# The reduced adjacency of a graph kernel: one wide product for up to four blocks of the unturned removal

## The chip, the cores and the metric

The kernel runs on one core of one Trainium2 chip. The metric is the device time of one execution in microseconds. The profile shows the core's engines: PE (TensorE's products, with PEld for its weight loads), DVE (VectorE), ACT (ScalarE), POOL (GpSimd) and SP, which here only issues DMAs.

## The reference, cut to what matters

Sixteen graphs of 1024 nodes with 64 features go through four layers. The first layer drops some neighbours and then takes, for every node and feature, weighted quantiles over the neighbours that are left; the other three layers are message passing, a second message passing and an attention. The change is in how the first layer's reduced adjacency is built:

```python
adj_ = jnp.where(eye, 1.0, adj)
neigh = (adj_ > 0) & ~eye
ni = neigh.astype(jnp.int32)
rank = jnp.cumsum(ni, axis=-1) - ni
nb = ni.sum(-1)
skip = jnp.maximum(jnp.where(nb > T, (nb + K - 1) // K, 1), 1)
sk = skip[:, :, None]
rem = neigh & (sk > 1) & (rank % sk == sk - 1) & mask[:, :, None]
rem = rem | jnp.swapaxes(rem, 1, 2)
adj_d = jnp.where(rem, 0.0, adj_)
nd = adj_d > 0
```

An edge is taken out when either of its two rows takes it out, so each block of the result needs the removals of its own row and those of the mirrored block, turned.

## The kernel before

The graphs go through in eight pairs. For a pair there are three kinds of work. `neighbours` builds the reduced adjacency of each of its two graphs, stored turned (`ndT`, L935 to L958), and counts its rows (L962). `sort_pair` sorts the pair's features on DVE (L791 to L793, then backwards L824 to L837). `select` reads both and finds the quantiles: products `comb` (L1120) of the reduced adjacency with weight tables `wt` (made on DVE at L998), then signs on ACT (L1175), maxima on DVE (L1191) and a second set of products `cand` (L1220). After it come `extras` and `layers` (the four layers' dense work of both graphs, with the attention at L1579 to L1609).

So the time has two kinds of stage in turn. In a selection stage PE, ACT and DVE work for `select` of pair k, and DVE also does the forward part of the sort of pair k+1. In a layer stage, the layers of pair k stand beside `neighbours` and the rest of the sort for pair k+1. The first 275 us hold `neighbours` and the sort of pair 0; the last pair's layers stand alone.

The order on each engine is not written out by hand. A scheduler places all instructions by priorities and modelled costs, and every engine then works through its own list in order. A kernel with fewer or shorter instructions at one place therefore gets another order around it.

In `neighbours`, each graph is cut into 8 x 8 blocks of 128 x 128. Rows of blocks t = 0 to 7 are handled in turn: ACT makes the row's removals `rem[:, t]` in three passes (L931, L932, L933), and then PE builds all blocks whose later index is t: the column of blocks (j, t) for j up to t, and the row (t, i) for i below t. A block is the sum, in PSUM, of three products: the turned neighbours (`ni` as stationary side against an identity), less the turned removals (`rem` against minus the identity, `minus_b`), less the removals of the mirrored block, which need no turning (`minus_b` as stationary side against `rem`). Diagonal blocks get the identity added. Up to four blocks share one PSUM tile `pk` of 512 columns, and ACT writes them out with a ReLU into `ndT` (L958). There are two such tiles (`bufs=2` of the pool `nbp`), shared with the transposes of the adjacency at L908.

The names of the layer stage that the prediction uses: L1460 are dense products with two weight tiles, L1469 and L1575 make the source side of the attention, L1579 and L1582 its destination side, L1595 and L1596 are the attention's exponential and sum, L1485 its gather products, L1607 turns the sum back and L1609 adds it to the features.

Of the kernel before, what the change touches and what calls it, by code (L numbers as in the profile page):

```python
# [9 lines left out]
F32 = mybir.dt.float32  # L10
# [7 lines left out]
AF = mybir.ActivationFunctionType  # L18
# [5 lines left out]
P = 128  # L24
# [18 lines left out]
def gnn_stack(ctx, tc, x, adj, nodemask, w, out):  # L43
# [10 lines left out]
    nc = tc.nc  # L54
# [10 lines left out]
    ident_b = const.tile([P, P], BF16, name="ident_b")  # L65
# [112 lines left out]
    minus_b = const.tile([P, P], BF16, name="minus_b")  # L178
# [519 lines left out]
    while size <= N:  # L698
        j = size // 2
# [182 lines left out]
    def neighbours(b, ndT, row10, qb, qz, nb, nbp):  # L882

        mask = maskf[:, b * NT : (b + 1) * NT]
        HT = NT // 2
        dq, coef = row10[:, :, :3], row10[:, :, 3:9].rearrange("p t (k s) -> p t k s", s=2)
        pad = 32
        wide = nb.tile([P, NT, pad + N], F8, name="ni")
        nc.gpsimd.memset(wide[:, :, pad - 1 : pad], 0.0)
        ni = wide[:, :, pad:]  # L890
        rem = nb.tile([P, NT, N], F8, name="rem")
        for t0 in range(0, NT, HT):
            cum = nb.tile([P, HT, N], F16, name="cum")
            for t in range(t0, t0 + HT):
                a = nb.tile([P, N], F32, name="a", bufs=2)
                nc.sync.dma_start(a, adj[b, t * P : (t + 1) * P, :])
                nc.vector.tensor_single_scalar(ni[:, t, :], a, 0.0, op=ALU.is_gt, saturate=False)
                nc.gpsimd.tensor_mul(  # L898
                    ni[:, t, t * P : (t + 1) * P], ni[:, t, t * P : (t + 1) * P], offdiag, saturate=False
                )  # L900

                nc.vector.tensor_tensor_scan(  # L902
                    cum[:, t - t0, :], ni[:, t, :], wide[:, t, pad - 1 : pad - 1 + N], 0.0, op0=ALU.add, op1=ALU.add
                )
                for q in range(0, NT, 4):
                    pt = nbp.tile([P, 4, P], F32, name="pk")
                    for k in range(4):
                        nc.tensor.transpose(pt[:, k, :], a[:, (q + k) * P : (q + k + 1) * P], ident)  # L908
                    at = nb.tile([P, 4, P], F32, name="at", bufs=3)
                    nc.scalar.copy(at, pt)  # L910
                    nc.scalar.dma_start(
                        a_d[b % 4, q : q + 4, :, t * P : (t + 1) * P].rearrange("j p n -> p j n"), at
                    )


            sk = nb.tile([P, 4, HT], F32, name="sk")
            nc.vector.tensor_tensor(sk[:, 2, :], cum[:, :, N - 1], ni[:, t0 : t0 + HT, N - 1], op=ALU.add)
            nbi = nb.tile([P, HT], I32, name="nbi")
            nc.vector.tensor_scalar_add(nbi, sk[:, 2, :], 2.0)
            nc.vector.tensor_single_scalar(nbi, nbi, 2, op=ALU.logical_shift_right)  # L920
            nc.vector.tensor_single_scalar(sk[:, 0, :], sk[:, 2, :], 2 * MAX_DEGREE, op=ALU.is_gt)
            nc.vector.tensor_mul(sk[:, 0, :], sk[:, 0, :], mask[:, t0 : t0 + HT])
            nc.vector.tensor_copy(sk[:, 1, :], nbi)
            nc.vector.scalar_tensor_tensor(sk[:, 1, :], sk[:, 1, :], 1.0, sk[:, 0, :], op0=ALU.add, op1=ALU.mult)
            nc.vector.tensor_scalar(sk[:, 2, :], sk[:, 1, :], -3.0, 4.0, op0=ALU.mult, op1=ALU.add)
            nc.vector.tensor_scalar_add(sk[:, 1, :], sk[:, 1, :], -1.0)
            nc.vector.scalar_tensor_tensor(sk[:, 3, :], sk[:, 1, :], -1.0, sk[:, 1, :], op0=ALU.mult, op1=ALU.mult)
            for t in range(t0, t0 + HT):
                k = t - t0
                sq = nb.tile([P, N], F32, name="sq")  # L930
                nc.scalar.activation(sq, cum[:, k, :], AF.Square, bias=sk[:, 2, k : k + 1], scale=1.0)  # L931
                nc.scalar.activation(sq, sq, AF.Square, bias=sk[:, 3, k : k + 1], scale=1.0)  # L932
                nc.scalar.activation(rem[:, t, :], sq, AF.Relu, bias=one, scale=-1.0, saturate=False)  # L933


                for blocks, to in (
                    ([(j, t) for j in range(t + 1)], ndT[:, : t + 1, t * P : (t + 1) * P]),
                    ([(t, i) for i in range(t)], ndT[:, t, : t * P].rearrange("p (i n) -> p i n", n=P)),
                ):
                    for n, (j, i) in enumerate(blocks):  # L940
                        if n % 4 == 0:
                            pk = nbp.tile([P, 4, P], F32, name="pk")
                        terms = [
                            (ni[:, i, j * P : (j + 1) * P], ident_b),
                            (rem[:, i, j * P : (j + 1) * P], minus_b),
                            (minus_b, rem[:, j, i * P : (i + 1) * P]),
                        ]
                        if i == j:
                            terms.append((ident_b, ident_b))
                        last = n % 4 == 3 or n == len(blocks) - 1  # L950
                        for m, (lhs, rhs) in enumerate(terms):
                            nc.tensor.matmul(  # L952
                                pk[:, n % 4, :], lhs, rhs, start=(n % 4 == 0 and m == 0),
                                stop=(m == len(terms) - 1 and last),
                            )
                        if last:
                            n0, m = n - n % 4, n % 4 + 1
                            nc.scalar.activation(to[:, n0 : n + 1, :], pk[:, :m, :], AF.Relu, saturate=False)  # L958
        pn = nbp.tile([P, 4, P], F32, name="pk")[:, 0, :NT]
        for i in range(NT):  # L960
            for j in range(NT):
                nc.tensor.matmul(  # L962
                    pn[:, i : i + 1], ndT[:, j, i * P : (i + 1) * P], ones_b[:, 0:1],
                    start=(i == 0 and j == 0), stop=(i == NT - 1 and j == NT - 1),
                )
        nc.gpsimd.tensor_copy(row10[:, :, 9], ids)

        last = nb.tile([P, NT], F32, name="last")
        nc.vector.tensor_scalar_add(last, pn, -1.0)
        lasts = last.rearrange("p (t o) -> p t o", o=1).to_broadcast([P, NT, 3])  # L970
        fr = nb.tile([P, 2, NT, 3], F32, name="fr")
        fi = nb.tile([P, NT, 3], I32, name="fi")
        nc.vector.tensor_mul(fr[:, 0], lasts, taus)
        nc.vector.tensor_scalar_add(fi, fr[:, 0], -0.4)
        nc.vector.tensor_copy(fr[:, 1], fi)
        nc.vector.tensor_sub(dq, lasts, fr[:, 1])
        nc.vector.tensor_scalar(qb, dq, -2048.0, -2048.0, op0=ALU.mult, op1=ALU.add)
        nc.vector.tensor_scalar(qz, dq[:, :, 0], -1.0, 1.0, op0=ALU.mult, op1=ALU.add)
        nc.vector.tensor_sub(fr[:, 0], fr[:, 0], fr[:, 1])
        nc.vector.tensor_mul(coef[:, :, :, 1], fr[:, 0], shares)  # L980
        nc.vector.tensor_sub(coef[:, :, :, 0], shares, coef[:, :, :, 1])
# [635 lines left out]
    def prepare(pr, nb, nbp):  # L1617

        made = []
        for i in range(2):  # L1620
            made.append((
                ndp.tile([P, NT, N], F8, name=f"ndT{i}"), ndp.tile([P, NT, 10], F32, name=f"row10{i}"),
                ndp.tile([P, NT, 3], F32, name=f"qb{i}"),
                ndp.tile([P, NT], F32, name=f"qz{i}"),
            ))
            neighbours(pr * 2 + i, *made[i], nb, nbp)
        return made
# [17 lines left out]
    for pr in range(pairs):  # L1645
# [17 lines left out]
        with ExitStack() as beside:  # L1663
# [5 lines left out]
            else:  # L1669
                nb_, nbp_ = side_pools()  # L1670
                nb, nbp = beside.enter_context(nb_), beside.enter_context(nbp_)
# [69 lines left out]
```

## Time and profile before

| what | value |
|---|---|
| median of 3 runs | 5758.06 us (5743.28 to 5765.65) |
| the profiled execution's own time | 5775.25 us |
| its span, first to last instruction | 5773.4 us |
| mean granted TensorE clock | 0.852 |
| PE busy | 4354.5 us, 75% |
| PE weight loads busy | 2724.9 us, 47% |
| DVE busy | 4997.9 us, 87% |
| ACT busy | 3813.2 us, 66% |
| POOL busy | 166.5 us, 3% |
| PE products, and as many weight loads | 45010 |

Busy time is a mean over stages. PE's products are pipelined, so that the length shown for one of them overlaps with the next one's; what a product costs is read from a run of them: length of the run by number. The view of busy time by stage gives, for a stretch of time, how long each engine was busy in it and with how many instructions. The chain of waits goes back from the last instruction to what released it each time; a line's share of it is time in which that line alone decided.

| the changed products before (L952) | count | mean length, ns | idle time of PE before them, us |
|---|---|---|---|
| turned neighbours, `ni` | 1024 | 247 | 108.0 |
| turned removals, `rem` stationary | 1024 | 251 | 175.6, waiting for L933 |
| unturned removals, `minus_b` stationary | 1024 | 251 | 0.0 |
| identity on the diagonal | 128 | 269 | 0.0 |

### The profile page before, as it was taken

To read this page: it belongs to the slowest core of one execution; us is meant where nothing else is said; L and a number is where in the kernel's file an instruction comes from. 1 tells how busy PE (TensorE), PEld (TensorE's weight loads), DVE (VectorE), ACT (ScalarE), POOL (GpSimd) and SP (SyncE) were. 2 spreads that over 40 slices of the span, in tenths; PEclk is the share of its full clock that TensorE was granted. 3 is DMA by queue.
4 is the path that set the end of the run, shared out by engine and by line. 5 is a ranking of instruction groups with operands and counts; after the bars stand their busy time and mean duration, and the time that the engine had idled before them with its cause. 6 is when DMAs were issued, how large, how long until landed. Compare 5 with 4: busy or idle time off the path is not lost.

```text
span 5773.4 us, 114332 instructions
## 1 busy us (share of the span) xinstructions
PE 4354.5 (75%) x45010; PEld 2724.9 (47%) x45010; DVE 4997.9 (87%) x13239; ACT 3813.2 (66%) x5763; POOL 166.5 (3%) x292
## 2 busy tenths in 40 slices
PE   1488677886778957788588885788767886779956
PEld 1355443554435544455434554355543554435642
DVE  9899888998889987999879988799888998878754
ACT  2587657775586855868568666687667866477835
POOL 3000000000000000000000000000000000000000
PEclk9699878997789978899779996899868997789967
DMA  4401264013731047210561115611255013630030
GB/s 129 127 27 41 88 208 134 26 37 107 227 96 35 28 133 232 68 37 23 158 225 53 41 45 175 199 38 40 82 173 173 28 40 90 212 113 18 10 101 5
DMA packets 519813, 551.45 MB, mean 96 GB/s; under 512 B 263297, under 2 KB 413057, under 8 KB 519265
## 3 DMA queue, kind: packets, MB, share of 16 engines
q1 hardware_dynamic: 376864, 459.65, 25.5%
q10 hardware_dynamic: 140064, 81.84, 4.6%
q8 instruction: 355, 5.82, 0.4%
q0 software_dynamic: 2336, 2.57, 0.2%
q14 instruction: 194, 1.58, 0.1%
HBM read 360.17 MB, written 183.76 MB: 94 GB/s over the span
## 4 chain that ended last, share of the span: by engine, by line
PE 34%; DVE 32%; ACT 19%; DMA 10%; issue 4%; POOL 0%; SPq 0%; ACTq 0%; DVEq 0%; POOLq 0%
PE comb L1120 11%; ACT sign L1175 6%; DVE y L1191 5%; PE cand L1220 5%; PE comb L1311 3%; PE bank L1485 3%; DVE cand L1228 3%; DMA a_d<-at 2%; ACT y L1128 2%; DVE cum L902 2%; DMA adjT<-a_d 2%; DVE s L793 1%; DVE s L792 1%; PE pk L952 1%; DVE swapped L791 1%
## 5 line engine op out<-in xcount | busy, mean ns | idle before, releaser
L1120 PE MATMUL comb<-wt,ndT 128*128 128x512 fp8e5 x6144 | 1435.6, 385 | 136.3 <-ACT sign L1175 112.1
L1128 ACT ACTIVATE y<-comb,qb 128x512 int16<-128x512 f32 x1152 | 743.5, 711 | 497.2 <-PE comb L1120 497.2
L1120 PEld LDWEIGHTS <-ndT 128*128 128x128 fp8e5 x6144 | 589.3, 98 | 852.9 <-issue 222.2
L1175 ACT ACTIVATE sign<-comb,lower 128x1024 fp8e5<-128x1024 int16 (+1 forms) x640 | 694.1, 1085 | 0.0
L1175 ACT ACTIVATE sign<-comb,half 128x1024 fp8e5<-128x1024 int16 (+1 forms) x640 | 688.9, 1076 | 0.0
L1220 PE MATMUL cand<-vtab,sign 128*128 128x48 f16 (+1 forms) x18432 | 668.4, 191 | 25.1 <-DVE agg L1097 15.2
L1220 PEld LDWEIGHTS <-sign 128*128 128x128 fp8e5 x18432 | 641.7, 96 | 85.1 <-issue 23.9
L1191 DVE TENSOR_TENSOR y<-y 128x512 uint16<-128x512 uint16 (+5 forms) x896 | 670.1, 790 | 10.5 <-PE comb L1173 10.0
L1228 DVE COPY_PREDICATED cand<-w_f,cand 128x256 f32<-128x256 uint16 (+1 forms) x1536 | 532.7, 378 | 84.1 <-PE cand L1220 81.7
L1173 PE MATMUL comb<-ident_b,y 128*128 128x128 bf16 x4608 | 307.0, 218 | 102.2 <-ACT sign L1175 70.2
L910 ACT COPY at<-pk 128x512 f32<-128x512 f32 x256 | 147.2, 585 | 351.6 <-PE pk L908 177.2
L952 PE MATMUL pk<-minus_b,rem 128*128 128x128 bf16 x1024 | 231.4, 251 | 175.6 <-ACT rem L933 175.6
L1173 PEld LDWEIGHTS <-y 128*128 128x128 bf16 x4608 | 284.8, 97 | 127.2 <-issue 127.1
L952 PE MATMUL pk<-ident_b,ni 128*128 128x128 bf16 x1024 | 227.0, 247 | 108.0 <-ACT ndT L958 63.4
L902 DVE TENSOR_TENSOR_SCAN cum<-ni 128x1024 f16<-128x1024 fp8e5 x128 | 292.3, 2284 | 17.7 <-POOL ni L898 14.4
L1485 PE MATMUL bank<-att,hs 128*64 128x512 f32 x512 | 195.7, 876 | 143.5 <-ACT hs L1601 143.5
L908 PE MATMUL pk<-ident,a 128*128 128x128 f32 x1024 | 188.0, 330 | 144.8 <-DMA a<-in_adj_dram 92.0
L998 DVE TENSOR_SCALAR wt<-node 128x2048 uint8<-128x2048 f16 x224 | 263.3, 1219 | 21.9 <-PE comb L1311 21.9
L1485 PE MATMUL bank<-adjT,nd 128*64 128x512 f32 x896 | 255.5, 638 | 29.7 <-DMA adjT<-a_d 29.2
L792 DVE TENSOR_TENSOR s<-s 128x384 f32<-128x384 f32 (+4 forms) x440 | 263.2, 598 | 0.0
L793 DVE TENSOR_TENSOR s<-s 128x384 f32<-128x384 f32 (+4 forms) x440 | 262.1, 596 | 0.0
L1186 DVE TENSOR_SCALAR y<-y 128x4608 int16<-128x4608 int16 x128 | 173.6, 1356 | 97.6 <-ACT y L1128 96.7
(382 smaller groups left out, 8340.5 us busy)
## 6 DMA issues: line engine op xcount, KB each, us to landing
adjT<-a_d SPq DMA_DIRECT2D x336, 512.0 KB
a<-in_adj_dram SPq DMA_DIRECT2D x128, 512.0 KB
a_d<-at ACTq DMA_DIRECT2D x256, 256.0 KB
m_d<-swapped SPq DMA_DIRECT2D x104, 512.0 KB
swapped<-m_d SPq DMA_DIRECT2D x104, 512.0 KB
n_d<-nat SPq DMA_DIRECT2D x128, 128.0 KB
x_d<-xr SPq DMA_DIRECT2D x48, 256.0 KB
comb_x<-x_d ACTq DMA_DIRECT2D x24, 512.0 KB
```

Source lines behind the costliest of these rows:

```text
L792: nc.vector.tensor_tensor(to_lo, lo, hi, op=ALU.max)
L793: nc.vector.tensor_tensor(to_hi, lo, hi, op=ALU.min)
L902: nc.vector.tensor_tensor_scan(cum[:, t - t0, :], ni[:, t, :], wide[:, t, pad - 1 : pad - 1 + N], 0.0, op0=ALU.add, op1=ALU.add)
L952: nc.tensor.matmul(pk[:, n % 4, :], lhs, rhs, start=(n % 4 == 0 and m == 0), stop=(m == len(terms) - 1 and last),)
L1120: nc.tensor.matmul(pw, ndT[:, j, t * P : (t + 1) * P], wt[1 + g8][:, j].rearrange("p w c -> p (w c)"), start=(j == 0), stop=(j == NT - 1),)
L1128: nc.scalar.activation(y[:, 0, chunks, at : at + 8 * d_].rearrange("p q (w d) -> p q w d", d=d_), pw.rearrange("p (w q d) -> p q w d", w=8 ...
L1173: nc.tensor.transpose(pt[:, q - q0, :], y[:, 0, q, :].bitcast(BF16), ident_b)
L1175: nc.scalar.activation(signs[tl][s][:, q0:q1, :], pt.bitcast(I16), AF.Sign, bias=before[s], scale=-1.0, saturate=False,)
L1191: nc.vector.tensor_tensor(v[:, :, :, :n], v[:, :, :, :n], v[:, :, :, n : 2 * n], op=ALU.max)
L1220: nc.tensor.matmul(cand[:, e, at : at + 12 * d_].rearrange("p (d l) -> p d l", l=12), signs[tl][sec][:, chunk, :], tab[:, q, :, half_ * 12 ...
L1228: nc.vector.copy_predicated(v[:, :, :, dst : dst + k], mk.to_broadcast([P, 2, C // 2, k]), v[:, :, :, frm : frm + k])
L1485: nc.tensor.matmul(po[to : to + C, :], lhs, rhs[:, f * HALF : (f + 1) * HALF], start=(j == 0), stop=(j == NT - 1))
```

## The change

The third product of each block is taken out of the loop over blocks. For each PSUM tile there is now one product with `minus_b` as stationary side and the removals of all its blocks, up to 512 columns, as moving side. It is the first of the tile and starts the accumulation; the other products follow and add to it.

```diff
-for blocks, to in (
-    ([(j, t) for j in range(t + 1)], ndT[:, : t + 1, t * P : (t + 1) * P]),
-    ([(t, i) for i in range(t)], ndT[:, t, : t * P].rearrange("p (i n) -> p i n", n=P)),
+for blocks, to, less in (
+    ([(j, t) for j in range(t + 1)], ndT[:, : t + 1, t * P : (t + 1) * P], rem[:, : t + 1, t * P : (t + 1) * P]),
+    (
+        [(t, i) for i in range(t)], ndT[:, t, : t * P].rearrange("p (i n) -> p i n", n=P),
+        rem[:, t, : t * P].rearrange("p (i n) -> p i n", n=P),
+    ),
 ):
-    for n, (j, i) in enumerate(blocks):
-        if n % 4 == 0:
-            pk = nbp.tile([P, 4, P], F32, name="pk")
-        terms = [
-            (ni[:, i, j * P : (j + 1) * P], ident_b),
-            (rem[:, i, j * P : (j + 1) * P], minus_b),
-            (minus_b, rem[:, j, i * P : (i + 1) * P]),
-        ]
-        if i == j:
-            terms.append((ident_b, ident_b))
-        last = n % 4 == 3 or n == len(blocks) - 1
-        for m, (lhs, rhs) in enumerate(terms):
-            nc.tensor.matmul(
-                pk[:, n % 4, :], lhs, rhs, start=(n % 4 == 0 and m == 0),
-                stop=(m == len(terms) - 1 and last),
-            )
-        if last:
-            n0, m = n - n % 4, n % 4 + 1
-            nc.scalar.activation(to[:, n0 : n + 1, :], pk[:, :m, :], AF.Relu, saturate=False)
+    for n0 in range(0, len(blocks), 4):
+        four = blocks[n0 : n0 + 4]
+        m = len(four)
+        pk = nbp.tile([P, 4, P], F32, name="pk")
+        nc.tensor.matmul(pk[:, :m, :], minus_b, less[:, n0 : n0 + m, :], start=True, stop=False)
+        for n, (j, i) in enumerate(four):
+            terms = [
+                (ni[:, i, j * P : (j + 1) * P], ident_b),
+                (rem[:, i, j * P : (j + 1) * P], minus_b),
+            ]
+            if i == j:
+                terms.append((ident_b, ident_b))
+            for k_, (lhs, rhs) in enumerate(terms):
+                nc.tensor.matmul(
+                    pk[:, n, :], lhs, rhs, start=False, stop=(n == m - 1 and k_ == len(terms) - 1)
+                )
+        nc.scalar.activation(to[:, n0 : n0 + m, :], pk[:, :m, :], AF.Relu, saturate=False)
```

## The prediction

> **What bounds the kernel now.** I read the page's chain of waits first, then busy time by stage, then the pieces of the chain that hold the changed line, and last the waits around it.
>
> ```profile
> span 5773.4 us, 114332 instructions
> ...
> PE 34%; DVE 32%; ACT 19%; DMA 10%; issue 4%; POOL 0%; SPq 0%; ACTq 0%; DVEq 0%; POOLq 0%
> PE comb L1120 11%; ACT sign L1175 6%; DVE y L1191 5%; PE cand L1220 5%; PE comb L1311 3%; PE bank L1485 3%; DVE cand L1228 3%; DMA a_d<-at 2%; ACT y L1128 2%; DVE cum L902 2%; DMA adjT<-a_d 2%; DVE s L793 1%; DVE s L792 1%; PE pk L952 1%; DVE swapped L791 1%
> ...
> L952 PE MATMUL pk<-minus_b,rem 128*128 128x128 bf16 x1024 | 231.4, 251 | 175.6 <-ACT rem L933 175.6
> ```
>
> No engine bounds the whole: the end is set by a chain that changes engine all the time, and the changed line, L952, holds 1% of it, about 58 us (between 29 and 87 by the rounding).
>
> ```profile
> 979.00:1360.00 381.00, 330.54 (x3854) 210.19 (x3853) 352.00 (x911) 277.81 (x453) 2.64 (x4) 0.94 0.10 31
> 1360.00:1683.00 323.00, 216.62 (x1782) 129.57 (x1781) 266.82 (x732) 199.88 (x271) 12.72 (x24) 0.74 0.59 183
> 1683.00:2057.00 374.00, 324.14 (x3848) 206.93 (x3846) 352.43 (x914) 276.81 (x451) 2.51 (x4) 0.96 0.10 32
> 2057.00:2382.00 325.00, 217.52 (x1778) 129.64 (x1779) 265.96 (x732) 200.13 (x271) 12.87 (x24) 0.75 0.58 181
> ...
> sum 2519.00, PE 300.91 PEld 241.46; mean PE 37.61 PEld 30.18
> ```
>
> The rows are stages: bounds, length, then busy time of PE, weight loads, DVE, ACT, POOL, the granted clock, DMA. A selection stage (375 us and more) and a stage of layers (about 320) alternate, seven times. L952 runs only in the layer stages and in the first 275 us. In a layer stage PE is busy for two thirds, DVE for five sixths: no engine is full, and what counts is who waits for whom. The last row is from the same view for L952 alone, over these eight stretches: it keeps PE busy for 300.9 us, so 58/301 = 19% of it lies on the chain.
>
> ```profile
> 163.55 2.33 PE pk L952 x20
> ...
> 300.82 5.33 PE comb L1120 x24
> ...
> 2828.53 2.21 PE pk L952 x19
> ...
> 2869.65 1.33 PE pk L952 x22
> ```
>
> These pieces of the chain give paces. A 128-column product of L952 takes 1.33/22 = 60.5 ns in a stretch at full clock and 2.33/20 = 117 ns where the clock is about half (granted 0.55 to 0.63 in the first stage). A 512-column product with an fp8 moving side takes 5.33/24 = 222 ns, or 55.5 per 128 columns. The group's mean of 251 ns is the length of one pipelined product; it isn't its price.
>
> **The change part by part.** *Removed:* 1024 products of 128 columns and their weight loads (64 blocks for each of 16 graphs). *Added:* 352 wide ones, 22 a graph: ten of 512 columns, four each of 384, 256 and 128. That is 672 products fewer, but the same 64 x 128 columns a graph. At full clock the saving is 1024 x (60.5 - 55.5) = 5.1 us of PE. At half clock, where no 512-column price is shown, twice 222 gives 111 per 128 columns: 1024 x (117 - 111) = 6.1 us. With 19% on the chain: **-1 us**. Upper bound of the gain: each of the 672 products worth a whole pace, 41 to 79 us of PE, of which 19% is 8 to 15 us. I take the low end, as the wide row is of the same engine and the same column count.
>
> One rule would say more. The Trainium skill, "TensorE: Matmul & The Clock Gate", section "Back-to-back issue gap", gives about 81 ns at 128 columns and about 131 at 512 for streams of load and product. With it 82.9 us would go and at most 352 x 131 = 46.1 come back, so 37 us of PE or 7 on the chain. This trace has 222 ns for the 512-column product, so the rule isn't followed.
>
> *The wait at the head of a group.* The block's `ni` product came first and needed no `rem`; the wide product comes first now and needs the fresh `rem` row, ACT's L933. Behind it stand the group's other products, and whatever layer work follows on PE; ACT's eviction L958 waits for the group.
>
> ```profile
> L952 PE MATMUL pk<-rem,minus_b x1024: 216/219/314, 105.0 to 5129.8; 128*128 128x128 fp8e5 x171
> ...
>   ACT rem L933: 373.3, 116
> ```
>
> PE waits for `rem` anyway, 58 times for a product (175.6 us) and 58 for a weight load. In the order of the program at most two `ni` products stand before such a wait. They move behind it: 58 x 2 x 60.5 to 117 = 7 to 14 us of PE, at 19% **+1 to +3 us**; where the scheduler had put nothing before the wait it is 0. I take +1. *Evictions* keep their number and shapes (352): 0; what covers this is only that ACT's work is unchanged. No DMA is added or removed.
>
> *The order.* The scheduler reorders around the shorter product list, and this is worth more than the products. Reading both programs' instruction orders: the first selection is unchanged on PE. In the old order the selection of pair 1 differs from those of pairs 2 to 5, which are alike; in the new one DVE's order from pair 1 on is the same in every cycle. The old pair-1 stage took 381 us against 374 and 375 in pairs 2 and 3: **-6.5 us**, if the order is what made it long.
>
> In each layer stage of the new order the neighbours' last products and their count (L962) stand before the second graph's attention instead of inside it, and four weight pieces (L998), not three, stand before the final sum L1609.
>
> ```profile
> 3035.39 0.17 DVE L1582 TENSOR_SCALAR fdst<-bank 128x8 f32<-128x8 f32 x1 [3.91 <-PE bank L1579]
> ...
> 3077.53 0.69 DVE L1609 TENSOR_TENSOR nd<-bank,xs 128x512 f32<-128x512 f32 x1 [1.38 <-PE bank L1607]
> ...
>   PE bank L1579: 25.0, 10
> ...
>   PE bank L1607: 12.2, 10
> ```
>
> The bracket is DVE's idle time before the instruction, the two last rows its totals for L1582 and L1609. DVE's stall at the stage's last L1609 is 1.51, 0.80, 1.24, 1.38, 0.50, 0.94 and 0 us in the seven stages, 6.4 in all. One more weight piece before it (1.2 us of DVE) covers it: **-6.4 us**. Late next are the weight pieces themselves, which DVE does one after the other, so nothing of it comes back.
>
> At L1582 I can't tell the sign. Between the second graph's layer-3 dense and the L1579 that DVE awaits, PE had 18 products of L952 and will have 17 + 4 + 8 = 29. Gain end: both waits vanish, 25.0 + 12.2 = 37 us (31 more than counted). Loss end: 11 more products at 117 ns, 1.3 us, and one more wait for an eviction, up to 3.4 us (the longest such wait of PE in one layer stage), so 4.7 us in each of seven stages, 33 us. I take 0, being about as near to one end as to the other.
>
> **Sum:** -1 + 1 - 6.5 - 6.4 = -13, with rounding **-14 us** against the span of 5773.4, so 5759.4. The profiled execution was 15 us above the median of the runs, 5758.06; scaled by 5759.4/5773.4 the forecast is **5744 us**, -0.24%.
>
> **The rivals.** *One: the second graph's chain queues behind the neighbours (slower).* Place: PE between L1460 and L1579 in every layer stage, with DVE's attention waiting at L1582. For it: the row of 3.91 us shows that DVE has nothing else to do there, and 29 products stand in front in place of 18. The Trainium skill's page named above, section "Step-by-step: what each phase is for", speaks for it too: only weight loads are pulled ahead, products stay in program order, so a product that waits holds all behind it; the rows only show PE idle at `rem`. Against it: the products moved forward were due later in the same stage. Price: 4.7 x 7 = 33 us, so 5777; it decides from 2 us a stage, and from 6.1 us a stage the kernel is over 0.5% slower. *Two: the earlier neighbours free the attention of its waits.* The 31 us above vanish as well: 5713. For it: DVE idles 55 us of a layer stage of 321. Against it: the waits at L1582 come from the second graph's own dense chain, which stays. *Three: PE's instruction count is what costs.* All 672 products lie on the path at a pace each, 41 to 79 us, middle 60: 5698. Against it: the row of 222 ns, and 1% of the chain. *That the change doesn't do what it says* can be excluded: the built program has the 352 wide products.
>
> **How the numbers follow.** Forecast 0.50 (its own range 5728 to 5762, from the pair-1 and L1609 terms being nothing or double), rival one 0.22, two 0.23, three 0.05. The range 5700 to 5788 takes in both ends of the L1582 term, 5713 and 5777, with some 11 us each for the spread of the runs shown (5743 to 5766). About 0.5%, 29 us, is what a measurement of this kernel can tell from no change. Below 5729: rival two 0.19, three 0.04, the forecast 0.06, so 0.29. Above 5787: half of rival one, 0.11, and 0.05 for a layer order that costs at places I haven't priced, 0.16. The rest, 0.55, is within.
>
> **What would show it.** In the profile after: 352 products of the wide form, the 512-column one at about 222 ns in dense stretches, and no 251 ns saved for each that went. The selection of pair 1 near 375 us. The last L1609 of a stage without a PE wait. L1582's wait for L1579: under 10 us in all speaks for rival two, 50 or more for rival one. Layer stages of 312 us or less, or 326 and more, would make the prediction wrong, since the sum leaves them within 2 us of 320. So would a selection stage that changes anywhere but in pair 1, as no changed line runs there.

## The result, and the profile after

| | kernel before | changed kernel |
|---|---|---|
| median of 20 runs, us | 5762.50 (5743.28 to 5777.65) | 5771.01 (5764.34 to 5787.46) |
| ratio, 95% interval | | 1.0023 (1.0013 to 1.0033) |
| span of the profiled execution, us | 5773.4 | 5766.4 |

The changed kernel is slower by 0.23%, about 13 us; 14 us less were forecast. The two profiles say the opposite of the medians: the profiled execution of before stood near the top of its range, that of the changed kernel in the lower half of its own. The executions of one kernel spread over 20 to 47 us, so two spans can't be set against each other here. Single stretches can, where they come back alike in every stage and every profile.

From the page of the changed kernel: the span, the chain of waits by engine and by line, and the two groups of the changed products (count, busy us, mean ns, idle time before them).

```profile
span 5766.4 us, 113021 instructions
...
PE 35%; DVE 29%; ACT 21%; DMA 10%; issue 3%; SPq 0%; POOL 0%; ACTq 0%; DVEq 0%; POOLq 0%
PE comb L1121 11%; ACT sign L1176 6%; DVE y L1192 5%; PE cand L1221 5%; PE bank L1486 4%; PE comb L1312 4%; DMA a_d<-at 3%; DVE cand L1229 3%; ACT y L1129 2%; DVE cum L902 2%; DMA adjT<-a_d 2%; DMA a<-in_adj_dram 2%; DVE wt L999 2%; ACT att L1596 2%; DVE s L793 1%
...
L947 PE MATMUL pk<-rem,minus_b 128*128 128x512 fp8e5 (+3 forms) x352 | 134.2, 383 | 214.8 <-ACT rem L933 174.1
...
L956 PE MATMUL pk<-minus_b,rem 128*128 128x128 bf16 x1024 | 187.7, 249 | 58.8 <-ACT rem L933 58.8
```

The 352 wide products are there (L947), and the two other products of a block are at L956; from L960 on every line number is one higher than before. The changed lines are no longer among those that the chain's row names. The chain itself is as mixed as it was.

In the answers on waits, for the lines of the layer stage that the prediction named (idle us of DVE before the line, and how often), before:

```profile
  PE bank L1579: 25.0, 10
...
  PE bank L1607: 12.2, 10
...
  ACT att L1595: 54.6, 49
```

and after:

```profile
  PE bank L1580: 11.2, 13
...
  PE bank L1608: 9.3, 4
...
  ACT att L1596: 71.6, 47
```

The waits for the attention's destination side (L1582, now L1583) and for the last transposes (L1609, now L1610) became shorter, by 13.8 and 2.9 us. DVE then waits that much longer for the attention's exponentials (L1596, now L1597): the three together were 91.8 us and are 92.1. Other profiles agree: 92.0 in a second one of the changed kernel (10.7, 9.1 and 72.2), 89.8 to 95.8 in five more of the kernel before. A wait that only moves to a later line of the same stage gives no time back.

### The profile page after: what moved, and what is told of

The parts are those of the page before. It is cut to its first block, busy times and chain, and to the rows that moved or that the text cites. A ratio compares the mean times of both kernels' runs of the same rounds, so it can differ in the third digit from the quotient of the medians.

```text
span 5766.4 us, 113021 instructions
## 1 busy us (share of the span) xinstructions
PE 4325.9 (75%) x44338; PEld 2688.1 (47%) x44338; DVE 5003.6 (87%) x13239; ACT 3813.5 (66%) x5763; POOL 168.6 (3%) x292
## 4 chain that ended last, share of the span: by engine, by line
PE 35%; DVE 29%; ACT 21%; DMA 10%; issue 3%; SPq 0%; POOL 0%; ACTq 0%; DVEq 0%; POOLq 0%
PE comb L1121 11%; ACT sign L1176 6%; DVE y L1192 5%; PE cand L1221 5%; PE bank L1486 4%; PE comb L1312 4%; DMA a_d<-at 3%; DVE cand L1229 3%; ACT y L1129 2%; DVE cum L902 2%; DMA adjT<-a_d 2%; DMA a<-in_adj_dram 2%; DVE wt L999 2%; ACT att L1596 2%; DVE s L793 1%
## 5 line engine op out<-in xcount | busy, mean ns | idle before, releaser
L947 PE MATMUL pk<-rem,minus_b 128*128 128x512 fp8e5 (+3 forms) x352 | 134.2, 383 | 214.8 <-ACT rem L933 174.1
L956 PE MATMUL pk<-minus_b,rem 128*128 128x128 bf16 x1024 | 187.7, 249 | 58.8 <-ACT rem L933 58.8
```

## The experiments

The instruction order of the changed kernel differs from that of before in three places that can be had one by one, since the scheduler reacts to single tiles of the products. *Y*: the layer stages, where neighbours' last products and the end of the sort stand elsewhere around the attention. *Z*: the second products of pair 1's selection. *X*: the backward exchanges of the sort on DVE, some loads on SP, and, as it turned out, a handful of products of the layer stage on PE. The variants keep the old product (`old`) for some tiles:

```diff
+old = <condition>
+if not old:
     nc.tensor.matmul(pk[:, :m, :], minus_b, less[:, n0 : n0 + m, :], start=True, stop=False)
...
     (rem[:, i, j * P : (j + 1) * P], minus_b),
 ]
+if old:
+    terms.append((minus_b, rem[:, j, i * P : (i + 1) * P]))
...
-    pk[:, n, :], lhs, rhs, start=False, stop=(n == m - 1 and k_ == len(terms) - 1)
+    pk[:, n, :], lhs, rhs, start=(old and n == 0 and k_ == 0), stop=(n == m - 1 and k_ == len(terms) - 1)
```

| kernel | condition for the old product | wide products | order | ratio to before, 95% |
|---|---|---|---|---|
| a_again | never | 352 | X, Y, Z | 1.0027 (1.0012 to 1.0042) |
| order_only | not (b odd and t in (4, 5)) | 56 | Y, Z | 0.9998 (0.9980 to 1.0016) |
| products_only | b odd and t in (4, 5) | 296 | X, Z | 1.0036 (1.0021 to 1.0051) |
| image0_only | b odd | 176 | X | 1.0022 (1.0009 to 1.0036) |
| b_again | always | 0 | as before | 1.0002 (0.9987 to 1.0017) |
| image0_kept | not (b even and t >= 2) | 152 | as before | 0.9984 (0.9967 to 1.0000) |
| exch_order | not (b even and t in (1, 4)) | 40 | X | 1.0025 (1.0009 to 1.0040) |
| no_exch | b even and t == 1 | 336 | Y in part, Z | 0.9980 (0.9964 to 0.9996) |

**First four: order or products?** The theory was that the loss comes from the layer stages' new order, the rival that the products themselves cost it.

a_again: 

> The changed kernel once more, unaltered, for a second profile and as the yardstick on the same chip as the next three. Both theories expect the ratio already measured, 1.0023 (1.0013 to 1.0033), some 8 to 19 us above the kernel before. By the theory of the order (the new place of the second image's products has the layer stage issued in another order, and that order is the dearer one), the layer stages of pairs 0 to 6 in this profile are again about 302 to 306 us with more of them near 306 than near 301, and the selection of pair 1 again some 10 us shorter than the 397 us before. By the theory of the products (the 352 wide products and their wait at the head of a group cost the time themselves) the loss is spread over all stages in which neighbours' products run.

order_only: 

> Only tiles 4 and 5 of the second image of each pair have the wide product: 7 wide products a pair, 56 in all, in place of 20 narrow ones; the other 864 of 1024 narrow products stay. The instruction order of the layer stages and of pair 1's selection becomes that of the changed kernel (19 of TensorE's other 41,535 instructions stand elsewhere than there by more than two places, against 1082 from the kernel before); only the sort's exchanges on VectorE keep the order of before. Theory of the order: the loss is there nearly whole, ratio 1.0010 to 1.0035 (5768 to 5783 us if the kernel before takes 5762). Theory of the products: 56 of 352, so 16% of the loss, ratio 1.0000 to 1.0006.

products_only: 

> The reverse: every product is wide but those of tiles 4 and 5 of the second image of each pair (296 wide products, 160 narrow ones left of 1024). The layer stages keep the order of the kernel before; pair 1's selection has the order of the changed kernel, and so have the sort's exchanges. Theory of the order: without the dearer layer stages the gain in pair 1's selection (some 10 us of the 12 that the two profiles show) is what is left, ratio 0.9975 to 0.9995, layer stages near 301 to 305 us as before. Theory of the products: 296 of 352, so 84% of the loss, ratio 1.0008 to 1.0030.

image0_only: 

> Only the first image of each pair has the wide products (176 of 352). Layer stages and all selections keep the order of before; only the sort's exchanges and, with them, some loads on SP stand a few places elsewhere (805 of VectorE's 13,887 instructions by more than two places). Theory of the order: nothing that matters is moved, ratio 0.9990 to 1.0007, and pair 1's selection stays near 397 us. Theory of the products: half of the loss, ratio 1.0006 to 1.0017.

My theory fell. order_only, with the layer stages' order of the changed kernel, loses nothing; products_only and image0_only lose as much as the changed kernel or more. Two things speak against the plain rival too: 176 wide products cost about as much as 352, and what the three slow kernels share besides wide products is order X.

**Next four: products or exchanges?** In X a backward exchange and some loads stand 3 to 30 places elsewhere. Tiles 1 and 4 of the first image, 5 wide products a pair, are enough for it (exch_order), and it goes when tile 1 alone is left old (no_exch).

b_again: 

> The kernel before once more, unaltered, as its own measure: a ratio whose interval holds 1 (every theory), and a second profile, to see whether the 397 us of pair 1's selection come back or belonged to that one execution.

image0_kept (152 wide products, not the 160 that the text says): 

> Wide products in tiles 2 to 7 of the first image of each pair alone: 160 of the 176 that image0_only had, and every other engine instruction in the order of the kernel before (VectorE 7 of 13,887 moved by more than two places, TensorE none, SP 11 DMAs of 1663). The sort's exchanges, which image0_only and products_only had moved, stay. Theory of the products, which the last four kernels left standing: 160 of 176 of image0_only's loss, ratio 1.0008 to 1.0030. Theory of the exchanges (the loss belongs to the sort's exchanges and the loads on SP issued in another order, which the changed kernel, products_only and image0_only share and order_only has not): ratio 0.9990 to 1.0008.

exch_order: 

> Wide products only in tiles 1 and 4 of the first image of each pair: 5 a pair, 40 in all, in place of 96 narrow ones. The sort's exchanges on VectorE and the 4x24 loads of vtab on SP stand as in image0_only (25 of 13,887 VectorE instructions and one DMA of 1663 differ from it by more than two places), the layer stages as before. Theory of the exchanges: the whole loss of image0_only, ratio 1.0010 to 1.0035. Theory of the products: 40 of 176 of it, ratio 0.9997 to 1.0008.

no_exch: 

> The changed kernel, with tile 1 of the first image of each pair alone put back to narrow products (336 of 352 wide products stay). That gives the sort's exchanges and the loads on SP their order of before; the layer stages have an order of their own, between the two kernels' (465 of TensorE's instructions moved from before, 646 from the changed kernel). Theory of the exchanges: no loss, ratio 0.9975 to 1.0007, about 14 us under the changed kernel. Theory of the products: 336 of 352 of the loss, ratio 1.0012 to 1.0040.

The three variants came out on the side of the theory of the exchanges (image0_kept, at 0.9984, a little under its 0.9990 to 1.0008), and none on that of the products: 40 wide products with order X lose 0.25%, 152 with the old order and 336 without X lose nothing. So the loss goes with X. What in X it is, the layer stages show. From the timeline of PE: start, length, line, operation, count, and in brackets PE's idle time before it. First the kernel before, pair 2:

```profile
2208.15 2.08 PE L1469 MATMUL bank<-srcT,l0w_t 64*128 64x512 f32 x4 [0.57 <-ACT srcT L1436]
2210.16 1.11 PE L1432 MATMUL bank<-ident,nd 128*128 128x128 f32 x4
2211.20 0.60 PE L1449 MATMUL bank<-l0b,ones 3*128 3x512 bf16 x1
2211.73 2.82 PE L1504 MATMUL bank<-l0w,two 128*128 128x64 f32 x12
2214.35 2.02 PE L1443 MATMUL bank<-hT,l1w_d 128*128 128x512 f32 x2
2216.30 0.60 PE L1449 MATMUL bank<-l1b,ones 3*128 3x512 bf16 x1
2216.83 1.11 PE L1504 MATMUL bank<-l0w,two 128*128 128x64 f32 x4
```

and the changed kernel, pair 2:

```profile
2191.03 2.07 PE L1470 MATMUL bank<-srcT,l0w_t 64*128 64x512 f32 x2
2193.03 1.11 PE L1433 MATMUL bank<-ident,nd 128*128 128x128 f32 x4
2194.08 2.07 PE L1470 MATMUL bank<-srcT,l0w_t 64*128 64x512 f32 x2
2196.09 0.60 PE L1450 MATMUL bank<-l0b,ones 3*128 3x512 bf16 x1
2196.62 0.69 PE L1505 MATMUL bank<-l0w,two 128*128 128x64 f32 x2
2197.10 2.02 PE L1444 MATMUL bank<-hT,l1w_d 128*128 128x512 f32 x2
2199.05 0.60 PE L1450 MATMUL bank<-l1b,ones 3*128 3x512 bf16 x1
2199.59 3.25 PE L1505 MATMUL bank<-l0w,two 128*128 128x64 f32 x14
```

These are the second image's layer-0 products (`halves_of(l0w1_t, ...)`, which uses L1469 too). One product takes rows 0 to 63 of the contraction, the other rows 64 to 127, each recorded as two instructions. Next to each other they took 2.08 us together. With the four transposes of the first image between them, each took 2.07 us. So they ran side by side as neighbours in PE's list, and one after the other with other products between them. In the Trainium skill, "TensorEngine Tiling (Array Packing)", section "Key Properties", tiles of the array are said to work independently of each other; 2.08 us for two against 2.07 for one agrees.

The views of busy time agree, each from the start of the pair to the end of the last of these 28 records, first before, then the changed kernel. The columns are bounds, length, busy time of PE, weight loads, DVE, ACT and POOL, then the granted clock:

```profile
2208.15:2217.94 9.79, 9.79 (x30) 5.58 (x31) 3.00 (x7) 5.75 (x9) 1.62 (x3) 0.50 0.19 55
...
2191.03:2202.84 11.81, 11.81 (x29) 6.09 (x30) 4.78 (x10) 6.15 (x9) 1.98 (x3) 0.50 0.15 48
```

The same 28 records stand in both (a product of the neighbours overlaps the bounds here and there), at the same clock, so the 2 us are the pair's. PE has no gap in this stretch, and DVE waits for its end. From the timeline of DVE, its two instructions at `x1` (L1511, now L1512), first image and second image of pair 2, before:

```profile
2202.07 0.69 DVE L1511 TENSOR_TENSOR xs<-bank,mask 128x512 f32<-128x512 f32 x1 [2.86 <-PE bank L1504]
...
2217.99 0.69 DVE L1511 TENSOR_TENSOR xs<-bank,mask 128x512 f32<-128x512 f32 x1 [6.77 <-PE bank L1504]
```

and after:

```profile
2185.02 0.69 DVE L1512 TENSOR_TENSOR xs<-bank,mask 128x512 f32<-128x512 f32 x1 [2.85 <-PE bank L1505]
...
2202.87 0.69 DVE L1512 TENSOR_TENSOR xs<-bank,mask 128x512 f32<-128x512 f32 x1 [6.89 <-PE bank L1505]
```

From one to the other, 15.92 us became 17.85. The waits in brackets hardly differ, because DVE does three instructions of the sort more in the longer stretch, and its L897 is longer there; only the distance of the two starts shows the loss. It was taken from every profile, for pairs 0 to 6:

| kernels | stages with the pair apart | stretches, us | sum of seven, us |
|---|---|---|---|
| before, b_again and four more profiles | 1 (pair 0) | 17.91, then 15.91 or 15.92 or (8 of 36) 12.86 to 13.08 | 107.4 to 113.4, mean 109.5 |
| order_only, image0_kept | 1 (pair 0) | as before | 110.5, 107.3 |
| no_exch | 1 (pair 0) | 17.91, then 12.58 to 13.08 | 94.3 |
| changed, a_again, products_only, image0_only, exch_order | 7 | 17.84 or 17.85, all 35 | 124.9 or 125.0 each |

**Four more: the pair alone.** The edit traces the two products together at high priority, and nothing else:

```diff
-for f, po in halves_of(l0w1_t, transposed(o0, "srcT")):
+o0t = transposed(o0, "srcT")
+with tc.high_priority():
+    both_l0 = list(halves_of(l0w1_t, o0t))
+for f, po in both_l0:
     nc.scalar.activation(hid[:, f, :], po, AF.Relu, bias=l0b1, scale=1.0)
```

exch_adj: 

> exch_order with one thing more: the two products of l0w_t of a layer stage (one for each 64 rows of the contraction) are traced together at high priority, so that they stand next to each other on TensorE in all 16 images. exch_order has transposes of the other image between them in 7 of 16, the kernel before in 1 of 16. Against exch_order VectorE and SP keep their order whole; TensorE has 21 instructions moved by more than two places, ScalarE 1. Theory of the split pair (side by side the two took 2.08 us, apart 2.07 us each, and VectorE waits for it): the stretch from x1 of the first image to x1 of the second falls from 17.85 us in pairs 0 to 6 to 12.6 to 15.9, and the ratio from 1.0025 to 0.9980 to 1.0003. Rival, the rest of the exchanges' order (the loads of vtab on SP 8 to 30 places earlier, exchanges a few places later on VectorE): the loss stays, 1.0010 to 1.0035.

after_adj: 

> The changed kernel with the same edit: all 352 wide products and the two products of l0w_t side by side in all images. Its layer stages then take an order of their own (654 of TensorE's instructions moved against the changed kernel, 473 against the one before). Theory of the split pair: 7 stretches of 17.85 us become 12.6 to 15.9, 14 to 37 us less, ratio 0.9960 to 1.0000 in place of 1.0023 to 1.0027. Rival (the wide products or another part of the new order cost the time): 1.0010 to 1.0035.

no_exch_adj: 

> no_exch (336 wide products, ratio 0.9980) with the same edit, which there heals pair 0 alone, the one stage where no_exch still has the pair apart (17.91 us). Theory of the split pair: 2 to 5 us less than no_exch, ratio 0.9960 to 0.9990. Every other theory: as no_exch, 0.9964 to 0.9996; the stretch of pair 0 tells.

b_adj: 

> The kernel before with the same edit, as control: only pair 0's stage has the pair apart there (17.91 us), and nothing else is moved (3 instructions of TensorE, 1 of ScalarE). Theory of the split pair: 2 to 5 us less in pair 0's stretch, ratio 0.9980 to 1.0003. What after_adj gains over this one is the wide products' own worth.

| kernel | median, us | ratio to before, 95% | sum of seven stretches, us |
|---|---|---|---|
| before, same chip | 5750.31 | | |
| exch_adj | 5742.65 | 0.9983 (0.9968 to 0.9998) | 98.4 |
| after_adj | 5739.13 | 0.9986 (0.9973 to 1.0000) | 92.5 |
| no_exch_adj | 5741.80 | 0.9983 (0.9967 to 1.0000) | 92.7 |
| b_adj | 5756.70 | 1.0006 (0.9992 to 1.0020) | 108.5 |

exch_adj against exch_order settles it: no instruction of DVE and no load on SP stands more than two places elsewhere (on PE products around the pair do, on ACT one eviction), the pair is together, and the ratio, each time to the kernel before on the same chip, falls from 1.0025 to 0.9983. That is some 24 us; the stretches of the two profiles lose 26.5. Of these 14.0 are the pair's own, seven stretches of 17.85 us against 15.85 where the clock stays at half; the other 12.6 come from four stretches of the short kind, as this one profile happened to have them. From PE's timeline of exch_adj, pair 2:

```profile
2190.03 2.01 PE L1474 MATMUL bank<-srcT,l0w_t 64*128 64x512 f32 x4 [0.46 <-ACT srcT L1441]
2191.98 0.66 PE L1437 MATMUL bank<-ident,nd 128*128 128x128 f32 x4
2192.82 0.37 PE L1454 MATMUL bank<-l0b,ones 3*128 3x512 bf16 x1 [0.18 <-ACT two L1508]
2193.12 1.55 PE L1512 MATMUL bank<-l0w,two 128*128 128x64 f32 x12
```

The four records stand in one row again. This is a stretch of the short kind, 12.51 us: after the pair all products run at about twice the pace (1.55 us for the twelve that took 2.82), and the granted clock from the pair's start on is 0.86 in the mean:

```profile
2190.03:2196.49 6.46, 6.27 (x31) 3.40 (x32) 4.35 (x10) 5.10 (x9) 2.16 (x3) 0.86 0.28 82
```

Three tests say less. With b_adj the edit shows no gain of its own: pair 0's stretch fell from 17.91 to 15.92 us, but the ratio, 1.0006, lies above the range expected. no_exch_adj and no_exch can't be told apart in time, though pair 0's stretch fell from 17.91 to 12.97 us. after_adj, the change with the pair kept together, is 21 to 24 us quicker than the changed kernel by the ratios to before (0.9986 against 1.0023 and 1.0027) and quicker than before at the very edge of its interval. Its layer stages have an order of their own, though (L1582's wait is 25.4 us as before, not 11.2), so it is the weaker test of the pair. Nor does it show what the wide products are worth against b_adj: in the same two profiles the stretches differ by 16 us.

**Four more profiles of the kernel before**, one execution each:

b_look1: 

> The kernel before, one more profile of four. If the loss is the pair's time alone, pairs 1 to 6 take 15.92 us each but for one or two, and 6 x 1.93 = 11.6 us is what the changed kernel loses there. If the chance of the short kind matters too, executions near or under the median (5750 to 5762) have three or more stretches of 12.5 to 13.1 us, and those 10 us above it none or one; each is worth 2.9 us.

b_look2: 

> As b_look1: the number of short stretches among pairs 1 to 6, 0 to 2 if the pair's time alone is the loss, 3 or more in a fast execution if the chance of the short kind matters.

b_look3: 

> As b_look1: 0 to 2 short stretches, or 3 and more in a fast execution.

b_look4: 

> As b_look1: 0 to 2 short stretches, or 3 and more in a fast execution.

They had 1, 2, 2 and 1 short stretches at 5763.1, 5772.2, 5769.3 and 5769.0 us. So 15.92 us is the rule in the kernel before, and most of what the changed kernel loses in these stretches is the pair's own 1.93 us a stage. None of the four was a quick execution, so whether the quick ones have more short stretches stays open.

## Why the prediction was wrong

*Products, -1 us: right in kind.* In a dense stretch at full clock a 512-column product keeps PE 0.21 us (profile of a_again, timeline of PE), and the narrow ones beside it start every 0.056 us:

```profile
3710.41 0.38 PE L947 MATMUL pk<-rem,minus_b 128*128 128x512 fp8e5 x1
3710.62 0.22 PE L956 MATMUL pk<-ident_b,ni 128*128 128x128 bf16 x1
3710.68 0.22 PE L956 MATMUL pk<-minus_b,rem 128*128 128x128 bf16 x1
```

Four narrow ones are 0.22 us, so a wide one saves next to nothing. image0_kept, the wide products in the old order, is 0 to 19 us quicker, which holds the -1 and can't say more. Rival three, the instruction count, would have shown a gain of 60 us and is out.

*Head of a group, +1 us: not contradicted.* PE's idle time before these products for want of `rem` rose from 175.6 to 232.9 us, more than the 7 to 14 us that I had. image0_kept, with 152 wide products, loses nothing by it.

*Pair 1's selection, -6.5 us: the size came, the reason didn't.* From the last L1609 of the stage before to the last product of `cand` it took 391.3 to 398.3 us in six profiles of before, 394.5 in the mean, and 385.1 us in both of the changed kernel: -9.4 us. But products_only, whose products stand there in the new order, took 394.8 us. The views of busy time, with the number of PE's products in the first brackets: before, products_only, the changed kernel.

```profile
978.14:1375.40 397.26, 343.65 (x4102) 221.68 (x4100) 364.80 (x939) 282.97 (x461) 3.63 (x7) 0.94 0.13 41
...
979.39:1374.16 394.77, 340.69 (x4101) 220.00 (x4100) 366.65 (x943) 282.83 (x461) 3.75 (x7) 0.95 0.13 42
...
980.10:1365.20 385.10, 332.84 (x4079) 217.08 (x4078) 360.55 (x938) 280.19 (x457) 3.48 (x7) 0.96 0.14 42
```

In the changed kernel 22 products of `comb` more had already run before that L1609, some 5 us at 222 ns each, and so they did in all six kernels that took 382.8 to 389.4 us: the bound has moved. From pair 0's last `cand` to pair 1's, where no bound moves, it took 694.8 to 707.7 us in six profiles of before (mean 700.7) and 691.1 and 695.3 in the changed kernel: -7.5 us, hardly clear of the spread. Nor was the old stage long for its order: over the six profiles pair 1's selection is no longer than pair 2's (394.5 against 395.1). The 381 against 374 came from one profile and bounds set by hand. That the size fits is luck, as far as it is clear of the spread at all.

*The last L1609, -6.4 us: the wait went, the time didn't.* In the seven stages this wait fell from 6.4 to 1.0 us, as forecast; after the change it is 1.00 us in pair 0 and nothing from pair 1 on:

```profile
980.08 0.69 DVE L1610 TENSOR_TENSOR nd<-bank,xs 128x512 f32<-128x512 f32 x1 [1.00 <-PE bank L1608]
...
1666.52 0.68 DVE L1610 TENSOR_TENSOR nd<-bank,xs 128x512 f32<-128x512 f32 x1
```

All of L1609's waits together fell by 2.9 us, since the first image of pair 0 has 3.19 for 0.34, and with the 13.8 us of L1582 they came back at the attention's exponentials. There the prediction had said that nothing of it comes back. order_only has the same shift (12.4, 9.2 and 71.6 us) and neither gains nor loses. That also ends rival two: the waits did become shorter, and nothing was gained. Rival one named the right side and stage, but not the place: the products between L1460 and L1579 hold nobody longer than before.

*The step that failed is "The order".* It said that in each layer stage the neighbours' last products and four weight pieces had moved, weighed only these, and took 0 for the rest of the stage. It left out six places of PE's order, one in each of pairs 1 to 6 (pair 0 had the pair apart before), where the second half of L1469 stands four places later and the first image's L1443 five places earlier. I had read where much work went, and no move as short as four places. The price is 125.0 - 109.5 = 15.5 us: 1.93 in each of pairs 1 to 6, 11.6 in all, and the rest the short stretches that the pair apart never has. The prediction kept 0.05, for more than 5787 us, for "a layer order that costs at places I haven't priced"; this is one.

The prediction's sum is -12.9 us by its terms, which rounds to -13 and not to -14, and the forecast's own range is 3 and 5 us wider than its two terms make it (5731 to 5757); neither changes the sign. With the stretch it is -7.5 + 15.5 = +8 us. The medians differ by 8.5 us (20 runs) and 11.5 us (a_again), the ratios by 7 to 24 with their intervals. This agreement is weak: the terms come from single executions, and all six profiled executions of before were slower than its median, with spans of 5768.5 us in the mean against 5766.6 in the two of the changed kernel. What made the typical execution of before quicker than these wasn't traced. That the pair apart costs time stands on exch_adj against exch_order.

Of the signs that were set, the pace of the wide product came as said, the stage's last L1609 lost its wait in six of the seven stages, and L1582's wait, 11.2 us, reached neither bound. With bounds set by hand the layer stages took 318 to 325 us, but pair 1's took 312, a sign against the prediction by its own words. It says little: from the last `cand` to the last L1609 that stage took 301.8 us, and 298.4 to 307.2 in six profiles of before. None of these signs looks at the stretch that decided.

## What to carry to other kernels

When a scheduler reorders around an edit, look for pairs in the order: here two products on different rows of the array, which shared its time only while they stood next to each other. Ask of each such pair whether something now stands between them, however few places it moved, and tie it together in the source before judging the edit. And hold the order fixed when an edit's own worth is to be measured: here the same 40 wide products read 1.0025 with the pair apart and 0.9983 with the pair together.

## What the runs showed of the hardware that I had not expected

At a granted clock of 0.50, two 64-row products took 2.08 us together and 2.07 us each alone.

The clock of PE stayed at half through long work without a gap. In the kernel before, PE works from 2208.15 to 2217.94 us without idling, at a granted clock of 0.50; with the pair apart that held in all 35 stretches, over some 11.8 us each. In 8 of 36 stretches of the kernel before, and in most of no_exch and after_adj, the clock went to 1.00 after the first few us of the same program. The Trainium skill, "TensorE: Matmul & The Clock Gate", section "Part 1: The HAM clock gate", has the clock go to full after one busy window of about 3.4 us, by a window that runs freely. The traces fit the free-running window: in all 18 of them every change of the granted clock lies on a grid of 3.41 us, whole multiples of it from the others. The 9.8 and 11.8 us at half pace don't fit the length.

The grid also tells the two kinds apart in the kernel before. The 8 short stretches are those whose pair starts between 0.20 us before a point of the grid and 0.31 us after it; in the 28 others it starts 0.54 to 2.87 us after one. Of the 35 stretches with the pair apart, 8 begin in that same range, and in none did the clock go up. In no_exch and after_adj, which have other work around it, the short kind also begins up to 1.6 us after a point. What the clock counts isn't shown.
